# Projecting ten row tiles in five pairs with seven block products instead of eight

## The chip, the cores and the metric

The kernel runs on one core of one Trainium2 chip. A core has five engines that run side by side, each with its own queue of instructions: TensorE (PE, matrix products; its loading of weights is listed as PEld), VectorE (DVE), ScalarE (ACT), GpSimd (POOL) and SyncE (SP), which here issues most of the DMAs. Matrix products are written to PSUM, eight banks of 512 f32 columns on 128 partitions; everything else lies in SBUF. All data here are f32.

The metric is the device time of one execution in microseconds. All times below are microseconds unless they are marked ns.

## The reference

There are 16 sequences. Each has 100 rows `x` of 640 values and 722 context rows of 384 values; the last four context rows are the extra tokens. With 8 heads of 80 values the reference computes, per sequence:

```python
enc, ca = ctx[:, :718, :], ctx[:, 718:, :]
hs   = mha(x @ Wq, enc @ Wk, enc @ Wv)           # main attention
q1   = einsum('btc,th->bch', ca, Wq_ca)[:, indices]   # 100 of 384 rows
h1   = mha(q1, x, x)                             # "first" softmax of the side branch
hs2  = mha(h1 @ Wq, ca @ Wk_ca, ca @ Wv_ca)      # "second" softmax, four keys
out  = (hs + hs2) @ Wout + b_out + x
```

The last line is what the change is about: 1600 rows of 640 values times a 640 x 640 matrix.

## The kernel before

**Batches.** The loop at line 1233 runs over the 16 sequences `b`. A batch makes the scores of its 718 keys in three groups of two blocks (`scores`, line 629), their maximum over all keys (`larger`, `Maximum`), then `st - max` and the exponentials in three parts (`subtract`, `exponential`), the sums of the exponentials (`r_ps`, line 1413), their inverse (`divide`, line 976) and the values (`a_ps`, line 1431). Inside the same batch the keys of the next one (`Keys`, line 487, and `last_keys`, line 619) and the values of this one (`Values`, line 444) are projected. Both already use a block scheme with fewer products, for which GpSimd prepares thirteen sums of the next encodings (`enc_sums`, line 515). Every odd batch also makes the queries of the next two (`queries`, line 565).

**The side branch** is the class `Second` (line 761). `scores1` makes 100 x 800 scores on GpSimd in `e1` with the help of a scratch tile `product`; `softmax1` takes their maximum on VectorE in steps (transpose, reduce, four small reductions twice, copy, transpose) and subtracts it; `exponentials1` is ScalarE's; `softmax2`, `scores2` and `softmax3` follow in the next batch. `spread2` sends the 32 probabilities of a row through DRAM so that they come back spread over all partitions in `pb`, and `values2` (line 912) multiplies and adds them on GpSimd to `hs2`.

**The output.** The 1600 rows are cut into 13 tiles: eleven of 128 rows, one of 64 and one of 128 (`OC`, line 33). A tile's rows, transposed, are collected in `hsT_r` (five chunks of 128 values by 128 rows), because a batch has 100 rows and a tile 128; `ENDS` (line 36) holds the batch in which a tile's last row is made. One batch later `place` (line 1026, GpSimd) multiplies by the inverse and adds `hs2`, `add_bias` adds the bias to the tile's rows of `x` in `xn`, and `project` (line 1051) makes two halves of 320 columns from five chunks each, ten matmuls of 128 x 128 by 128 x 320. VectorE adds the result to `xn`, SP stores it. `O_AFTER` (line 37) says for each tile after which batch it is projected: tiles 0 to 9 in batches 2, 3, 4, 6, 7, 8, 10, 11, 12 and 14. The last three tiles are done in batch 15 and after the loop.

**Order.** From line 1232 on the order of every engine's instructions, SP's DMAs among them, is the order of the program text (`manual_schedule`); before that, in the preparation, a scheduler orders them by when they are ready. An engine runs its queue in order, so an instruction that waits holds up all behind it. `wait_for(ins, seen)` makes an instruction wait for the last maximum of the batch.

**Room.** `xT` (transposed `x` of two batches), `ca`, `mb` and `ys` (four small or middle tiles of the side branch) have two buffers, `hsT` two, `xn` two, `pb` one and `product` one. PSUM is used in three sets of two: `ps2` (pairs of banks, `pair`), `psk` and `ps1`. `most` (128 x 800) holds the running maximum of the scores; its rows from 96 on are set to a low value once and then overwritten up to row 120.

These lines stand at the end of a batch before the change:

```python
        if 0 < b < B - 2:
            enc_sums(enc_next)
        if b % 2 and b + 1 < B:
            ...
                queries(p + 1, xT, tiles, n)
        if 0 < b < B - 1:
            second.exponentials1()
```

Ahead of them, in the branch of batches 1 to 14, stand `last_keys`, the load of the rest of the encodings, `second.softmax1()` and `last.project()`; behind them come the matmuls of `r_ps`, `divide`, the matmuls of `a_ps` and `keep`.

Of the kernel before, what the change touches and what calls it, by code (L numbers as in the profile page):

```python
# [33 lines left out]


ENDS = [(lo + n - 1) // S for lo, n in OC]
O_AFTER = [b + 1 if b % 2 == 0 and b + 1 not in ENDS else b for b in ENDS]
HT = NH * T


# [113 lines left out]
def kernel(  # L154
# [73 lines left out]
    def load_x(p):  # L228
        xT = inp.tile([P, 2, HC, S], F32, tag="xT", name=f"xT_{p}")
        nc.sync.dma_start(  # L230
            out=xT, in_=xt[2 * p : 2 * p + 2].rearrange("b p c s -> p b c s")
        )
        return xT
# [46 lines left out]
    kT = const.tile([P, HC, 3, KT], F32, name="kT")  # L280
    wout_sb = const.tile([P, HC, H], F32, name="wout_sb")
    bias = const.tile([P, H], F32, name="bias")

    wvca_sb = enc_tile("wvca").rearrange("p f k -> p (f k)")[:, : CC * H].rearrange(
        "p (c n) -> p c n", c=CC
# [34 lines left out]
    xT = inp.tile([P, 2, HC, S], F32, tag="xT", name="xT_0")  # L320
    in_order(nc.sync.dma_start(out=xT, in_=xt[0:2].rearrange("b p c s -> p b c s")))
    ca_0 = small.tile([S, T, S], F32, tag="ca", name="ca_0", bufs=2)
# [69 lines left out]
    e1 = const.tile([P, ROWS], F32, name="e1")  # L392
    nc.gpsimd.memset(e1[96:, :], LOW)

    ys = []
    for j in range(2):
        y = const.tile([S, NH, HT + 1], F32, name=f"y_{j}")
        nc.gpsimd.memset(y[:, :, HT:], 1.0)
        ys.append(y)


    def first_values(i, enc, engines, halves=(0, 1), get=psum):
# [335 lines left out]
    def load_m(b, behind=None):  # L738
        if b < 2:
            return lambda c: m_sb[c][:, b * HT : (b + 1) * HT]  # L740
        mb = small.tile([P, HC, HT], F32, tag="mb", name=f"mb_{b}", bufs=2)
# [19 lines left out]
    class Second:  # L761


        def __init__(self, b, xT, ca=None):
            self.b, self.xT = b, xT[:, b % 2]
            self.top = None

            self.ca = ca
            if ca is not None:
                return  # L770
            self.ca = small.tile([S, T, S], F32, tag="ca", name=f"ca_{b}", bufs=2)
            nc.sync.dma_start(
                out=self.ca, in_=cas[b].unsqueeze(0).to_broadcast([S, T, S])
            )
# [24 lines left out]

        def copy(self):  # L800
            b, y_ps = self.b, self.y_ps
            self.y = ys[b % 2]
# [109 lines left out]
        def values2(self, behind=None):  # L912

            b = self.b
            pb = self.pb.rearrange("p c (t q) -> p c t q", t=T)
            self.hs2 = hs2_tile(f"hs2_{b}")[:, : HC * S].rearrange("p (c q) -> p c q", c=HC)
            for t in range(T):
                to = self.hs2
                if t:
# [3 lines left out]
                first = nc.gpsimd.tensor_tensor(  # L923
                    to, pb[:, :, t], va.to_broadcast([P, HC, S]), ALU.mult
                )
                if t:
                    nc.gpsimd.tensor_tensor(self.hs2, self.hs2, to, ALU.add)  # L927
# [9 lines left out]
    spare = []  # L937

    class Last:

# [5 lines left out]
        def load(self, behind=None):  # L946

            self.xn = {}
            for r, (lo, n) in enumerate(OC):
                if self.b != O_AFTER[r]:  # L950
                    continue
                xn = self.xn[r] = spare[1] if r == len(OC) - 1 else xn_tile(f"xn_{r}")
                rows = x.rearrange("b s n -> (b s) n")[lo : lo + n]
# [91 lines left out]
        def put(self):  # L1045
            for to, o_ps, o_v in self.due:
                nc.vector.tensor_tensor(to, o_ps, to, ALU.add)
                nc.sync.dma_start(out=o_v, in_=to)
            self.due = []

        def project(self, halves=(0, 1), apart=False, put=True):
            for r, xn in self.xn.items():
# [180 lines left out]
    for b in range(B):  # L1233
# [40 lines left out]
        nc.vector.tensor_tensor(most[:KN], st[0][:, 0], st[0][:, 1], ALU.max)  # L1274
        st.append(scores(b, 1, tiles))
# [12 lines left out]
        if b == 0:  # L1288
# [25 lines left out]
            keys(m_next)  # L1314
            enc_sums(enc_next)
            now.values2()
            second.softmax1(4)
        elif b + 1 < B:
            vv = Values(b, e_in)

            def both(n):
                vv.go(n)
                kk.go(n)

            second.scores1(seen)
            last.load(seen)
            if b + 2 < B:
                m_next = load_m(b + 2, seen)
                keys(m_next)
# [36 lines left out]
            if b + 2 < B:  # L1366
                enc_next = load_rest(b + 2, enc_next)
            second.softmax1()
            last.project()
        else:  # L1370
            vv = Values(b, e_in)
            last.place()
            last.load()
            mine.load()
            last.add_bias(seen)
            top.go(3)
            vv.go(3)
# [12 lines left out]
            vv.go(5)  # L1390
            last.put()
            vv.go(1)
            subtract(1)
            exponential(2)
            vv.go(1)
            exponential(1)
            vv.go(5)
        if 0 < b < B - 2:
            enc_sums(enc_next)
        if b % 2 and b + 1 < B:  # L1400
            xT, tiles = xT_at[0], queries_tiles(p + 1)
            for n in range(HC):
                queries(p + 1, xT, tiles, n)
        if 0 < b < B - 1:
            second.exponentials1()

        rests = psum1(f"r_ps_{b}")[:, : 2 * S].rearrange("p (e q) -> p e q", e=2)
# [33 lines left out]
            mine.keep(wides)  # L1441
        else:
            mine.finish(wides)
        if b == 0:
            second.softmax1()
            second.exponentials1()
        last = mine

    last.project(apart=True)
# [50 lines left out]
```

## Time and profile before

| what | us |
|---|---|
| median of three runs | 934.5 (933.68 to 935.29) |
| the profiled execution itself | 933.61 |
| its span in the trace | 931.9 |
| even batch with a projection (from `s_ps` to `s_ps`) | 52.9 |
| odd batch with queries, without a projection | 56.0 |
| odd batch with queries and a projection | 61.4 |

The span runs from the first to the last instruction in the trace; the execution's own time has 1.7 more around it. The lengths of batches are differences between the starts of the first scores in the chain in order of time (381.17 to 434.10, 325.16 to 381.17 and 434.10 to 495.49).

How to read the lines of the profile that follow. A line of the groups has the source line, the engine, the operation, output<-inputs, shapes, the count, the busy time in all and the mean of one in ns, then the engine's idle time before it and what ended most of that. A line of the timeline has start, length, engine, line, operation and shapes; the square bracket is the idle time of the engine just before, and what ended it. A line of the chain in order of time has start, length, engine and group, merged over neighbours. SPq is SP's queue of DMA issues. "x20" at a matmul counts instructions; a product of f32 matrices is two of them, each with its weight load.

### The profile page before, as it was taken

To read this page: it belongs to the slowest core of one execution; us is meant where nothing else is said; L and a number is where in the kernel's file an instruction comes from. 1 tells how busy PE (TensorE), PEld (TensorE's weight loads), DVE (VectorE), ACT (ScalarE), POOL (GpSimd) and SP (SyncE) were. 2 spreads that over 40 slices of the span, in tenths; PEclk is the share of its full clock that TensorE was granted. 3 is DMA by queue.
4 is the path that set the end of the run, shared out by engine and by line. 5 is a ranking of instruction groups with operands and counts; after the bars stand their busy time and mean duration, and the time that the engine had idled before them with its cause. 6 is when DMAs were issued, how large, how long until landed. Compare 5 with 4: busy or idle time off the path is not lost.

```text
span 931.9 us, 26041 instructions
## 1 busy us (share of the span) xinstructions
PE 923.7 (99%) x11183; PEld 784.3 (84%) x11183; DVE 650.8 (70%) x1087; ACT 375.4 (40%) x649; POOL 573.3 (62%) x622
## 2 busy tenths in 40 slices
PE   9999999999999999999999999999999999999998
PEld 6997879788897888988788887987889888897865
DVE  3848894886919678495955959578592876939583
ACT  2234534434334344533425434344532444434350
POOL 5649857576645865467682666756665566556444
PEclk9999999999999999999999999999999999999999
DMA  8712262051400504132131411314131050401212
GB/s 258 241 39 67 54 129 72 20 145 29 108 26 23 144 12 109 29 83 74 35 106 30 112 45 42 76 25 130 44 98 36 19 146 15 107 14 50 63 52 64
DMA packets 68667, 69.16 MB, mean 74 GB/s; under 512 B 26056, under 2 KB 62344, under 8 KB 68552
## 3 DMA queue, kind: packets, MB, share of 16 engines
q1 hardware_dynamic: 67224, 66.18, 26.9%
q8 instruction: 88, 1.44, 0.7%
q10 hardware_dynamic: 864, 0.98, 0.3%
q0 software_dynamic: 464, 0.34, 0.1%
q14 instruction: 27, 0.22, 0.1%
HBM read 61.81 MB, written 8.94 MB: 76 GB/s over the span
## 4 chain that ended last, share of the span: by engine, by line
PE 96%; DVE 2%; DMA 1%; issue 0%; ACT 0%; POOL 0%; SPq 0%; DVEq 0%; ACTq 0%
PE s_ps L643 12%; PE v_psA L468 10%; PE v_psB L468 8%; PE kT_ps L593 8%; PE k_psA L499 7%; PE q_ps L569 7%; PE a_ps L1431 7%; PE o_ps L1061 7%; PE k_psB L499 6%; PE r_ps L1413 4%; PE v_psC L468 3%; PE k_psC L499 3%; PE v_ps L409 2%; PE y_ps L782 2%; PE v_psD L468 2%; PE v_psE L468 2%
## 5 line engine op out<-in xcount | busy, mean ns | idle before, releaser
L817 POOL TENSOR_TENSOR e<-ca,g 100x800 f32<-100x800 f32 x64 | 99.4, 1564 | 156.8 <-DVE most L1263 140.4
L534 POOL TENSOR_TENSOR enc<-enc 128x240 f32<-128x240 f32 x135 | 96.5, 725 | 21.6 <-DMA enc<-in_enct 14.6
L468 PE MATMUL v_psA<-wv_sb,enc 128*120 128x320 f32 x352 | 109.6, 434 | 0.2 <-ACT st L671 0.2
L923 POOL TENSOR_TENSOR hs<-pb,vaT 128x500 f32<-128x500 f32 x64 | 73.0, 1150 | 53.7 <-DMA pb<-wide_d 51.2
L643 PE MATMUL s_ps<-qp,kT 32*120 32x100 f32 x3072 | 97.9, 263 | 0.0
L643 PEld LDWEIGHTS s_ps<-qp,kT 32*120 32x120 f32 x3072 | 95.0, 180 | 2.1 <-issue 0.2
L824 POOL TENSOR_TENSOR e<-e,e 100x800 f32<-100x800 f32 x48 | 90.6, 1887 | 3.8
L468 PE MATMUL v_psB<-wv_sb,enc 128*120 128x320 f32 x296 | 91.9, 433 | 0.0
L499 PE MATMUL k_psA<-enc,wk_sb 128*128 128x240 f32 x360 | 87.9, 367 | 1.1 <-DVE kT L439 1.0
L1274 DVE TENSOR_TENSOR most<-st 120x800 f32<-120x800 f32 x16 | 17.6, 1100 | 100.8 <-ACT st L671 100.8
L1251 DVE TENSOR_TENSOR st<-st,over 120x1600 f32<-120x1600 f32 x47 | 85.3, 1814 | 0.0
L499 PEld LDWEIGHTS k_psA<-enc,wk_sb 128*128 128x128 f32 x360 | 68.3, 190 | 18.0 <-DVE kT L439 1.3
L468 PEld LDWEIGHTS v_psA<-wv_sb,enc 128*120 128x120 f32 x352 | 63.4, 184 | 22.4 <-DVE vs L439 0.5
L1263 DVE TENSOR_TENSOR most<-most,st 120x800 f32<-120x800 f32 x64 | 65.7, 1027 | 22.8 <-ACT st L665 21.6
L1259 ACT ACTIVATE st<-st 120x1600 f32<-120x1600 f32 x48 | 73.9, 1540 | 8.2 <-DVE st L1251 7.7
L499 PE MATMUL k_psB<-enc,wk_sb 128*128 128x240 f32 x300 | 73.1, 367 | 0.1
L468 PEld LDWEIGHTS v_psB<-wv_sb,enc 128*120 128x120 f32 x296 | 54.3, 184 | 21.7 <-DVE vs L439 0.4
L1028 POOL TENSOR_TENSOR hsT<-hsT,ratio 128x500 f32<-128x500 f32 (+22 forms) x26 | 20.5, 788 | 83.0 <-DVE st L1251 74.0
L927 POOL TENSOR_TENSOR hs<-hs,hs 128x500 f32<-128x500 f32 x48 | 68.0, 1416 | 3.8
L1431 PE MATMUL a_ps<-st,vs 120*64 120x100 f32 (+1 forms) x1536 | 69.5, 250 | 0.0
L569 PE MATMUL q_ps<-xT,wq_sb 128*128 128x200 f32 x400 | 69.1, 333 | 0.0
L1431 PEld LDWEIGHTS a_ps<-st,vs 120*64 120x64 f32 (+1 forms) x1536 | 66.4, 137 | 2.7 <-issue 2.4
(166 smaller groups left out, 1854.2 us busy)
## 6 DMA issues: line engine op xcount, KB each, us to landing
pb<-p_d SPq DMA_DIRECT2D x32, 400.0 KB
enc<-in_enct SPq DMA_DIRECT2D x30, 240.0 KB
enc<-in_enct SPq DMA_DIRECT2D x15, 360.0 KB
xT<-in_xt SPq DMA_DIRECT2D x8, 500.0 KB
rest<-in_enct SPq DMA_DIRECT2D x31, 120.0 KB
xn<-in_x SPq DMA_DIRECT2D x11, 320.0 KB
wide_d<-p_d SPq DMA_DIRECT2D x16, 200.0 KB
pb<-wide_d SPq DMA_DIRECT2D x16, 200.0 KB
```

Of the source, the lines that this page charges most:

```text
L468: nc.tensor.matmul(at[0][j][:KN, : H // 2], a_form(self.enc, f)[:, j * KN : (j + 1) * KN], wv_there.get(f, wv_sb[:, W_AT[f]]), start=first ...
L499: nc.tensor.matmul(at[:, i * KT : (i + 1) * KT], wk_sb[:, W_AT[f], i], a_form(self.enc, f), start=(first and i == 0), stop=last, skip_grou ...
L534: nc.gpsimd.tensor_tensor(out, left, right, op)
L569: nc.tensor.matmul(q_ps[:, : 2 * S].rearrange("p (j s) -> p j s", j=2), wq_sb[:, c, n * P : (n + 1) * P], xT[:, :, c, :], start=(c == 0), ...
L593: nc.tensor.matmul(bank[:, i * KT : (i + 1) * KT], weights[c], a_raw(enc, u, c), start=(i == 0 and c == 0), stop=(c == CC - 1), skip_group ...
L643: nc.tensor.matmul(s_ps[bank][:n, 256 * a + lo : 256 * a + lo + rhs.shape[-1]], kT[rows, c, u, j * KN : (j + 1) * KN], rhs, start=bank not ...
L817: first = nc.gpsimd.tensor_tensor(to, self.ca[:, t, :].unsqueeze(1).to_broadcast([S, NH, S]), g[:, :, t].unsqueeze(2).to_broadcast([S, NH, ...
L824: nc.gpsimd.tensor_tensor(e, e, to, ALU.add)
L923: first = nc.gpsimd.tensor_tensor(to, pb[:, :, t], va.to_broadcast([P, HC, S]), ALU.mult)
L1251: return engine.tensor_tensor(st[i], st[i], top.over[:KN].unsqueeze(1).to_broadcast([KN, 2, ROWS]), ALU.subtract,)
L1259: nc.scalar.activation(st[i], st[i], AF.Exp, scale=SCALE)
L1431: nc.tensor.matmul(wides[64 * e : 64 * e + 64, h // 2], slot(i, h, FIRST[e], 64), st[i // 2][: KEYS[i], i % 2, h * S : (h + 1) * S], start ...
```

## The change

It does four things.

1. **Pairs.** Tiles 0 to 9 are projected as five pairs, in batches 3, 6, 8, 11 and 13, the batch after the second tile's last row. With the two tiles' first four chunks as a 2 x 2 block matrix `A` and the first four chunks of `Wout` as a 2 x 2 block matrix `B`, Winograd's form of Strassen's scheme needs seven block products instead of eight; the fifth chunk is done as before. The sums of blocks of `A` are made per pair on GpSimd (`row_sums`, right behind `place`), into the room of `most` and in place; the sums of blocks of `B` once on VectorE (`out_sums`, at the end of batch 1), three into a new tile and one in place, whose block is loaded again in batch 14 (`again`).
2. **The block itself** (`project_pair`) uses a pair of banks and two single ones. VectorE adds partial sums to `xn` in the middle of the sums; in even batches the steps of `softmax1` are put between these additions. At its end GpSimd sets the rows of `most` again, ahead of `enc_sums`.
3. **Room.** `xT`, `ca`, `mb` and `y` get one buffer, `product` lies in the room of `pb`, `values2` works in place, `hsT` gets three buffers.
4. **Order.** The stores of a pair are kept and issued in the next batch behind its last maximum, ahead of that batch's load of `xn`. In even batches without a pair the second half of `softmax1` comes behind `keep`, and `exponentials1` in the next batch behind the first group of scores, as it was in batch 0.

```diff
-O_AFTER = [b + 1 if b % 2 == 0 and b + 1 not in ENDS else b for b in ENDS]
+NPAIRS = 5
+O_AFTER = [ENDS[r | 1] - (r + 1) % 2 for r in range(2 * NPAIRS)] + ENDS[2 * NPAIRS :]
+PAIRED = {ENDS[r + 1]: (r, r + 1) for r in range(0, 2 * NPAIRS, 2)}
...
-        return main.tile([P, HC, P], F32, tag="hsT", name=name, bufs=2)
+        return main.tile([P, HC, P], F32, tag="hsT", name=name, bufs=3)
...
-        xT = inp.tile([P, 2, HC, S], F32, tag="xT", name=f"xT_{p}")
+        xT = inp.tile([P, 2, HC, S], F32, tag="xT", name=f"xT_{p}", bufs=1)
...
-            self.ca = small.tile([S, T, S], F32, tag="ca", name=f"ca_{b}", bufs=2)
+            self.ca = small.tile([S, T, S], F32, tag="ca", name=f"ca_{b}")
...
-                    to = product_tile(f"hs2_{b}_{t}")[:, : HC * S]
-                    to = to.rearrange("p (c q) -> p c q", c=HC)
+                to = pb[:, :, t] if t else self.hs2
...
     def product_tile(name):
-        return main.tile([P, ROWS], F32, tag="product", name=name)
+        return pb_tile(name)[:, :ROWS]
+    def out_sums():
+        (b11, b12), (b21, b22) = w_there
+        for out_w, left, right in (
+            (wout_t[:, 0], b12, b11),
+            (b12, b22, b12),
+            (wout_t[:, 1], b22, wout_t[:, 0]),
+            (wout_t[:, 2], b21, wout_t[:, 1]),
+        ):
+            nc.vector.tensor_tensor(out_w, left, right, ALU.subtract)
...
+        def row_sums(self):
+            t0, t1 = (hsTs[r] for r in PAIRED[self.b])
+            room = most[:, : 6 * P].rearrange("p (i c s) -> p i c s", i=3, c=2)
+            self.s1, self.s2, self.s4 = (room[:, i] for i in range(3))
+            a11, a12, a21, a22 = t0[:, :2], t0[:, 2:4], t1[:, :2], t1[:, 2:4]
+            for to, left, right, op in (
+                (self.s1, a21, a22, ALU.add),
+                (a21, a11, a21, ALU.subtract),
+                (self.s2, self.s1, a11, ALU.subtract),
+                (self.s4, a12, self.s2, ALU.subtract),
+            ):
+                nc.gpsimd.tensor_tensor(to, left, right, op)
+        def project_pair(self, steps):
...
+            step()
+            product(y, t0[:, :2], b11, True)
+            product(z, t1[:, :2], t3, True)
+            add(x0[:, 0], y[:, : H // 2])
+            step()
+            product(y, self.s2, tt2)
+            add(x1, both[:, :, : H // 2])
+            step()
+            product(v, t0[:, 2:4], b21, True)
+            rest(v, t0, 0)
+            product(y, self.s1, tt1)
+            add(x0[:, 1], y[:, : H // 2])
+            step()
+            product(z, t1[:, 2:4], tt4)
+            rest(z, t1, 0)
+            add(x1[:, 0], z[:, : H // 2])
+            step(8)
+            product(w, self.s4, b22, True)
+            rest(w, t0, 1)
+            rest(y, t1, 1)
+            add(x0[:, 0], v[:, : H // 2])
+            add(x0[:, 1], w[:, : H // 2])
+            add(x1[:, 1], y[:, : H // 2])
+            nc.gpsimd.memset(most[96:, :], LOW)
+            held.extend((r, xns[r]) for r in (r0, r1))
...
             second.scores1(seen)
+            store(seen)
             last.load(seen)
+            if b == B - 2:
+                again()
...
             last.place(subtract(1))
+            if last.b in PAIRED:
+                last.row_sums()
             last.add_bias()
...
-            second.softmax1()
-            last.project()
...
-        if 0 < b < B - 2:
-            enc_sums(enc_next)
+        paired = 0 < b and last.b in PAIRED
+        late = b % 2 == 0 and not paired
+        if b < B - 1 and (b % 2 or late):
+            second.softmax1(4 if late else 8)
...
-        if 0 < b < B - 1:
+        if paired:
+            last.project_pair(None if b % 2 else second.softmax1)
+        if 0 < b < B - 2:
+            enc_sums(enc_next)
+        if b < B - 1 and not late:
             second.exponentials1()
...
-        if b == 0:
+        if b == 1:
+            out_sums()
+        if late and b < B - 1:
             second.softmax1()
-            second.exponentials1()
```

`product` and `rest` in `project_pair` are two matmuls over the two chunks of a block and one over the fifth chunk, each 128 x 128 by 128 x 320; `add` is one VectorE addition from PSUM into `xn`; `t3` is the block changed in place.

More of the change, by code (lines that the diff above doesn't have):

```diff
@@ L282 @@
     bias = const.tile([P, H], F32, name="bias")
+    wout_t = const.tile([P, 3, 2, H // 2], F32, name="wout_t")
+    w_there = [
+        [wout_sb[:, 2 * i : 2 * i + 2, k * (H // 2) : (k + 1) * (H // 2)] for k in range(2)]
+        for i in range(2)
+    ]
     wvca_sb = enc_tile("wvca").rearrange("p f k -> p (f k)")[:, : CC * H].rearrange(
@@ L319 @@
     load_first(0, CC, 0, slice(0, KT))
-    xT = inp.tile([P, 2, HC, S], F32, tag="xT", name="xT_0")
+    xT = inp.tile([P, 2, HC, S], F32, tag="xT", name="xT_0", bufs=1)
     in_order(nc.sync.dma_start(out=xT, in_=xt[0:2].rearrange("b p c s -> p b c s")))
-    ca_0 = small.tile([S, T, S], F32, tag="ca", name="ca_0", bufs=2)
+    ca_0 = small.tile([S, T, S], F32, tag="ca", name="ca_0")
     in_order(nc.sync.dma_start(out=ca_0, in_=cas[0].unsqueeze(0).to_broadcast([S, T, S])))
@@ L393 @@
     nc.gpsimd.memset(e1[96:, :], LOW)
[L395 to L399, printed above, removed]
+    y_there = const.tile([S, NH, HT + 1], F32, name="y")
+    nc.gpsimd.memset(y_there[:, :, HT:], 1.0)
     def first_values(i, enc, engines, halves=(0, 1), get=psum):
@@ L740, in load_m @@
             return lambda c: m_sb[c][:, b * HT : (b + 1) * HT]
-        mb = small.tile([P, HC, HT], F32, tag="mb", name=f"mb_{b}", bufs=2)
+        mb = small.tile([P, HC, HT], F32, tag="mb", name=f"mb_{b}")
         loaded = nc.sync.dma_start(
@@ L801, in copy @@
             b, y_ps = self.b, self.y_ps
-            self.y = ys[b % 2]
+            self.y = y_there
             nc.scalar.copy(
@@ L931, in product_tile, with again, store @@
     def product_tile(name):
-        return main.tile([P, ROWS], F32, tag="product", name=name)
+        return pb_tile(name)[:, :ROWS]
     hsTs = {}
     spare = []
+    def out_sums():
[7 more added lines that the diff above has]
+            nc.vector.tensor_tensor(out_w, left, right, ALU.subtract)
+    def again():
+        rows = wout.rearrange("(c e k) n -> e c k n", e=2, k=D)
+        for e in range(2):
+            nc.sync.dma_start(
+                out=w_there[0][1][64 * e : 64 * e + 64],
+                in_=rows[e, :2, FIRST[e] : FIRST[e] + 64, H // 2 :].rearrange(
+                    "c k n -> k c n"
+                ),
+            )
+    xns = {}
+    held = []
+    def store(behind):
+        while held:
+            r, xn = held.pop(0)
+            lo, n = OC[r]
+            stored = nc.sync.dma_start(
+                out=out.rearrange("b s n -> (b s) n")[lo : lo + n], in_=xn[:n]
+            )
+            wait_for(stored, behind)
     class Last:
@@ L952, in load @@
                 xn = self.xn[r] = spare[1] if r == len(OC) - 1 else xn_tile(f"xn_{r}")
+                xns[r] = xn
                 rows = x.rearrange("b s n -> (b s) n")[lo : lo + n]
@@ new lines, in project_pair, with product, rest, add @@
+        def project_pair(self, steps):
+            r0, r1 = PAIRED[self.b]
+            t0, t1 = hsTs[r0], hsTs[r1]
+            x0, x1 = (xns[r].rearrange("p (k d) -> p k d", k=2) for r in (r0, r1))
+            b11, t3 = w_there[0]
+            b21, b22 = w_there[1]
+            tt1, tt2, tt4 = (wout_t[:, i] for i in range(3))
+            both = pair(f"o_ps_{r0}")
+            y, z = both[:, 0], both[:, 1]
+            v, w = psumk(f"o_psv_{r0}"), psumk(f"o_psw_{r0}")
+            def product(bank, rows, weights, first=False, last=False):
+                for c in range(2):
+                    nc.tensor.matmul(
+                        bank[:, : H // 2],
+                        rows[:, c],
+                        weights[:, c],
+                        start=(first and c == 0),
+                        stop=(last and c == 1),
+                        skip_group_check=True,
+                    )
+            def rest(bank, rows, k, last=True):
+                nc.tensor.matmul(
+                    bank[:, : H // 2],
+                    rows[:, HC - 1],
+                    wout_sb[:, HC - 1, k * (H // 2) : (k + 1) * (H // 2)],
+                    start=False,
+                    stop=last,
+                    skip_group_check=True,
+                )
+            def add(to, left):
+                nc.vector.tensor_tensor(to, left, to, ALU.add)
+            def step(n=1):
+                if steps:
+                    steps(n)
+            step()
[23 more added lines that the diff above has]
+            held.extend((r, xns[r]) for r in (r0, r1))
@@ L1271 @@
         st.append(scores(b, 0, tiles))
-        if b == 0:
+        if b == 0 or late:
             now.exponentials1()
@@ L1316 @@
             now.values2()
-            second.softmax1(4)
         elif b + 1 < B:
@@ L1443 @@
             mine.finish(wides)
-        if b == 0:
+        if b == 1:
+            out_sums()
+        if late and b < B - 1:
             second.softmax1()
-            second.exponentials1()
         last = mine
```

2 lines of the change are left out of this document (removed).

## The prediction

> **What bounds the kernel now.** I read the page first, then the groups of instructions, then the chain in order of time, and last the timeline of single batches.
>
> ```profile
> span 931.9 us, 26041 instructions
> PE 923.7 (99%) x11183; PEld 784.3 (84%) x11183; DVE 650.8 (70%) x1087; ACT 375.4 (40%) x649; POOL 573.3 (62%) x622
> PE 96%; DVE 2%; DMA 1%; issue 0%; ACT 0%; POOL 0%; SPq 0%; DVEq 0%; ACTq 0%
> ```
>
> TensorE is busy for 99% of the span and holds 96% of the chain that ended last. A busy PE alone proves little, because ends of matmuls are modelled; the chain in order of time is better, since it shows when each group starts:
>
> ```profile
> 313.29 5.38 PE o_ps L1061 x20
> 318.67 2.21 PE r_ps L1413 x96
> ...
> 362.57 3.65 PE kT_ps L593 x18
> 366.22 8.46 PE q_ps L569 x50
> 374.68 2.22 PE r_ps L1413 x96
> ...
> 418.58 3.65 PE kT_ps L593 x18
> 422.23 5.38 PE o_ps L1061 x20
> ```
>
> Groups follow each other without a gap: 313.29 + 5.38 = 318.67, where `r_ps` starts. In batch 4 the projection is in that row, in batch 5 none stands between the keys and `r_ps` (only queries), in batch 6 it is there again. So whatever TensorE no longer does should come off the span, as long as the other engines keep up with the shorter batches.
>
> **The change, part by part.** *Products removed.* One tile costs 20 instructions (an f32 matmul is two) in 5.38, so one takes 5.38 / 20 = 0.269. Two tiles had 2 x 2 x 5 = 20 matmuls. The pair block has seven products of two chunks and four for the fifth chunk: 18. That is 36 instructions of the same form for 40, 36 x 0.269 = 9.68 instead of 10.76. Five pairs: 5 x 1.08 = **5.38 less**. Ten batches' blocks become five (batches 3, 6, 8, 11, 13), so batches 3, 6, 8 and 11 grow by 9.68 - 5.38 = 4.30 and 13 by 9.68, and batches 2, 4, 7, 10, 12 and 14 lose 5.38.
>
> *Handovers added.* Bank `y` is read by VectorE three times while TensorE goes on summing in it. This is new, so I lay the block into batch 6, the even case, where the steps of the softmax stand between the additions:
>
> ```profile
> 417.31 1.81 DVE L1251 TENSOR_TENSOR st<-st,over 120x1600 f32<-120x1600 f32 x1
> 419.04 1.00 DVE L706 STREAM_TRANSPOSE turned<-e 128x800 f32<-128x800 f32 x1
> 420.08 0.99 DVE L708 TENSOR_REDUCE quad<-turned 128x25 f32<-128x800 f32 x1
> 421.10 0.71 DVE L711 TENSOR_REDUCE side<-quad 32x25 f32<-32x25 f32 x4
> 421.85 1.32 DVE L718 TENSOR_REDUCE mx<-side 32x25 f32<-32x100 f32 x4
> 423.20 0.99 DVE L733 COPY spread<-mx 128x800 f32<-128x800 f32 x1
> 424.22 1.01 DVE L736 STREAM_TRANSPOSE over<-spread 128x800 f32<-128x800 f32 x1
> 425.26 0.99 DVE L834 TENSOR_TENSOR e<-e,over 100x800 f32<-100x800 f32 x1
> 427.72 0.82 DVE L1074 TENSOR_TENSOR xn<-o_ps,xn 128x640 f32<-128x640 f32 x1 [1.46 <-PE o_ps L1061]
> L1047 DVE TENSOR_TENSOR xn<-o_ps,xn 128x320 f32<-128x320 f32 x2 | 1.0, 488 | 0.8 <-PE o_ps L1061 0.8
> 89.40 1.08 PE L499 MATMUL k_psA<-enc,wk_sb 128*128 128x240 f32 x4 [0.97 <-DVE kT L439]
> 88.70 0.65 DVE L439 TENSOR_TENSOR kT<-k_psA,kT 128x480 f32<-128x480 f32 x1
> ```
>
> From matmul to addition: the projection ends at 427.61 and the addition starts at 427.72, 0.11 later; the last matmul's ending is modelled, so I allow 0.3. An addition of 320 columns takes 0.49, of 640 columns 0.82. From VectorE back to TensorE: the addition ends at 88.70 + 0.65 = 89.35, the matmul that waited starts at 89.40, 0.05 later. The block starts at 422.23. `y` is done at 423.31 and `z` at 424.38. VectorE has finished its first step at 420.04, so it adds `y` until 423.31 + 0.3 + 0.49 = 424.10, and TensorE may write `y` again at 424.15: 0.23 to spare, or none if the weights of that matmul must wait too, one instruction (0.27) ahead. Then VectorE's second step lasts to 425.1; `y` is done at 425.46, both banks are added until 426.6, and TensorE, with six instructions in `v`, comes back to `y` at 427.07: 0.4 to spare. The third step (2.0) ends at 428.6 and the third addition at 429.1; TensorE needs `y` again at 431.4 and `z` was free from 426.6. In odd batches no step stands between. So the cost lies between 0 (all fits) and 0.3 a pair (the allowance at the first point doubled); VectorE is idle when `y` comes, so I take a value near 0: 0.05 a pair, 0.25 in all.
>
> The rest of VectorE's work there is hidden by TensorE: its steps end at 432.6 and the three last additions at 434.1, before the inverse, which follows `r_ps` (431.9 + 2.2 = 434.1). ScalarE's exponential at 432.6 (0.87 long) is also done before that. Without this cover the additions would cost 1.5 a pair.
>
> *Less cover in batches 2, 4, 10, 12 and 14.* With the block gone, `r_ps` starts at 313.29 in batch 4. It needs the third pair of scores in its last third, at 313.29 + 2/3 x 2.21 = 314.8:
>
> ```profile
> 308.37 1.81 DVE L1251 TENSOR_TENSOR st<-st,over 120x1600 f32<-120x1600 f32 x1
> 310.28 1.54 ACT L1259 ACTIVATE st<-st 120x1600 f32<-120x1600 f32 x1
> ...
> 104.84 1.24 POOL L927 TENSOR_TENSOR hs<-hs,hs 128x500 f32<-128x500 f32 x1
> 105.08 1.85 DVE L1274 TENSOR_TENSOR most<-st 120x800 f32<-120x800 f32 x1 [2.53 <-ACT st L671]
> 161.84 0.99 DVE L1274 TENSOR_TENSOR most<-st 120x800 f32<-120x800 f32 x1 [6.20 <-ACT st L671]
> ```
>
> The exponential ends at 311.82, so 3.0 remain. Moving the second half of the softmax behind `divide` puts 1.01 + 0.99 of VectorE into the 6.20 in which it waits for the next scores, and its exponential (0.87) between two groups of ScalarE's copies of them; a bank is copied some 0.1 later. Cost 0, and 0.1 a batch at most.
>
> *GpSimd.* Four sums of 128x256 a pair, near the 128x260 row (0.74), make 2.9; the fill of `most` counts as a fifth, 0.74.
>
> ```profile
> L1028 POOL TENSOR_TENSOR hsT<-hsT,ratio 128x260 f32<-128x260 f32 x1 | 0.7, 740 | 5.3 <-DVE st L1251 5.3
> 419.47 2.02 POOL L923 TENSOR_TENSOR hs<-pb,vaT 128x500 f32<-128x500 f32 x2 [3.24 <-DMA pb<-wide_d]
> 427.22 1.27 POOL L927 TENSOR_TENSOR hs<-hs,hs 128x500 f32<-128x500 f32 x1
> 783.66 3.04 POOL L817 TENSOR_TENSOR e<-ca,g 100x800 f32<-100x800 f32 x2 [7.98 <-DVE most L1263]
> ```
>
> In batch 6 the sums fit into the 3.24 in which GpSimd waits for the spread probabilities. The fill waits for TensorE's last product (431.9), and behind it are queued the thirteen sums of the next encodings; they start at 432.7 instead of 428.5, where `values2` ends, 4.2 later. TensorE's next batch, and with it the maximum that `scores1` waits for, comes 4.3 later too, so that wait stays as it is. In an unpaired even batch the least wait before `scores1`, 7.98, shrinks by 5.38 to 2.6. So all of it costs 0; uncovered it would be 3.6 a pair. GpSimd and VectorE do hold each other up: `most` took 1.85 beside GpSimd's sum at 104.84 and 0.99 alone. Against a cost of 0 speaks a rule of the Trainium skill, page SBUF — State Buffer, section Who interferes with whom: a VectorE instruction with two inputs in SBUF and a GpSimd one that reads SBUF exclude each other for a whole instruction. By it the moved subtraction (0.99) would hold GpSimd up once a batch, and 1.6 of the 2.6 would remain, so the sum is the same and only the GpSimd rival below gains weight. The trace agrees, by the two rows of `most`.
>
> *Weight sums*, once, behind batch 1: four of 128x640, twice the 0.49 of 320 columns, so 3.9, or by the factor of the two rows of `most` (1.85 / 0.99) up to 7.3, of which the 6.20 before 161.84 hold all but 1.1; that 1.1 would make `scores1` late once, within the 7.98. Cost 0; without that cover 3.9 once.
>
> *Single buffers.* In the loop `xT`, `ca`, `mb` and `y` are written only after their last reader has long run, since that reader stands earlier in the same batch. `product` shares `pb`, whose other users are on the same GpSimd queue or follow it. The stores come behind the next maximum, two of them, ahead of `xn` and `mb`; `mb` is needed only after `scores1`, some 12 later. Cost 0. The start is different:
>
> ```profile
> 41.52 0.52 SPq L230 DMA_DIRECT2D xT<-in_xt  x1
> 42.09 0.40 SPq L772 DMA_DIRECT2D ca<-in_cas  x1
> 51.59 28.75 SPq L246 DMA_DIRECT2D enc<-in_enct  x6
> 78.63 1.72 SPq L246 DMA_DIRECT2D enc<-in_enct  x3
> 57.44 0.69 POOL L534 TENSOR_TENSOR enc<-enc 128x240 f32<-128x240 f32 x1 [14.56 <-DMA enc<-in_enct]
> 68.47 1.21 PE L782 MATMUL y_ps<-m,xT 128*100 128x96 f32 x10
> 80.21 1.54 POOL L817 TENSOR_TENSOR e<-ca,g 100x800 f32<-100x800 f32 x1
> 85.75 0.69 POOL L534 TENSOR_TENSOR enc<-enc 128x240 f32<-128x240 f32 x1
> 113.46 3.03 POOL L817 TENSOR_TENSOR e<-ca,g 100x800 f32<-100x800 f32 x2 [3.68 <-DVE most L1263]
> ```
>
> Now `xT_1` waits for the last reader of `xT_0` (to 69.68) and `ca_2` for that of `ca_1` (to 81.75). Batch 2's encodings, the second three of the six at 51.59, queue behind: from 78.6 to about 82.2. The first encodings took 57.44 - 51.59 = 5.9, so sums that start at 85.75 wait to about 88, 2.3 of the 3.68 that are free. Cost 0. TensorE's 0.97 of waiting at 89.40 lies in this stretch and may go or double, so -1 to +1 for the range.
>
> *The sum*, against the profiled execution's own 933.61 (its span 931.9 and 1.7 around it): 933.61 - 5.38 + 0.25 = 928.5. The median of the runs, 934.5, is 0.9 above that execution, so I predict **929.4**.
>
> **The rivals.** *A. The handovers take the gain back.* If VectorE answers a step late at two places of a block (0.3 and 0.5), a pair loses 0.8 and the five 4.0: 933.4. For it: the first handover has 0.23 or less. Against: VectorE is idle before it.
>
> *B. Slower: batch 1's encodings fall behind `xT_1` in SP's queue.* In the trace `xT` and `ca` stand ahead of them, at 41.52 and 42.09. If that order stays while `xT_1` waits to 69.68, the encodings leave 18.1 late, and their thirteen sums start at 75.5 and end some 10 later. TensorE wants them from 69.7 on, and GpSimd's `scores1`, queued behind all of them, makes the softmax behind it late: some 15 lost, 929.4 + 15 = 944. It decides as soon as the load of `enc_1` is issued after 69. Against: those loads stood behind only because their own buffer came free at 51.6, which is now earlier than the others' are.
>
> *C. GpSimd sets the pace in unpaired even batches.* If VectorE instructions that it did not meet before held it up for 4 in all (four of about 1.0), 1.4 beyond the reserve would be lost in each of five: 936.4. For it: 2.6 is the smallest reserve, and the rule above. Against: nothing of its work is added there.
>
> *D. No shorter block.* If 36 instructions with interrupted sums took the time of 40 (0.299 each), the gain would be nil: 934.7. Against: same shapes and same pitch.
>
> **How the numbers follow.** Forecast 0.78, A 0.09, B 0.06, C 0.04, D 0.03. About 0.2% (1.9 us: 932.6 to 936.4) is what a measurement can tell from no change. Faster is the forecast and a third of A: 0.81. Same is the rest of A and D: 0.09. Slower is B and C, as C's own 936.4 is the edge: 0.10. The forecast's own range is 928.2 (the wait at 89.40 gone) to 930.8 (it doubled, with 0.1 a pair); up to 932.4 it takes in the milder part of A.
>
> **What would show it.** Right: projection rows of 36 instructions in about 9.7, five times, with at most 0.3 of idle PE inside; kT followed directly by `r_ps` in batches 2, 4, 10, 12 and 14 with no wait for an exponential; `scores1` still waiting for `most` everywhere, by 2 to 3 after those batches; `enc` loads issued near 52 at the start. Wrong: PE waiting for `xn` additions by more than 0.3, `p2t` on VectorE waiting for `p_in` by more than now, or a first batch that is longer.

## The result, and the profile after

| kernel | median us | range | runs |
|---|---|---|---|
| before | 934.09 | 933.02 to 935.29 | 4 |
| after | 940.15 | 939.93 to 940.48 | 4 |

The ratio is 1.0065 with a 95% interval of 1.0047 to 1.0082: the change made the kernel slower by 6.1, where 5.1 less was forecast. The page of the changed kernel, its span, engines and the chain that ended last:

```profile
span 938.2 us, 26084 instructions
PE 921.5 (98%) x11163; PEld 777.7 (83%) x11163; DVE 660.2 (70%) x1116; ACT 374.8 (40%) x649; POOL 611.8 (65%) x646
PE 91%; DVE 6%; ACT 1%; issue 1%; POOL 0%; DVEq 0%; POOLq 0%; ACTq 0%
```

TensorE has 20 instructions fewer and is busy 2.2 less, but the chain has passed from TensorE to VectorE by some per cent. First, where: the starts of the first scores in the chain in order of time, before and then after.

```profile
157.60 7.28 PE s_ps L643 x240
210.85 7.28 PE s_ps L643 x240
272.24 7.28 PE s_ps L643 x240
```

```profile
157.63 7.28 PE s_ps L650 x240
205.17 7.28 PE s_ps L650 x240
273.34 7.28 PE s_ps L650 x240
```

Batch 2 takes 47.54 instead of 53.25, as it should (-5.71). Batch 3, with a pair block, takes 68.17 instead of 61.39: +6.78, where +4.30 was forecast. All batches, by what the change does in them, as differences from before. The column of the forecast holds the products alone, without the allowance of 0.25; the last two columns are experiments told below.

| stretch | forecast | after | two tiles | two tiles, `over` later |
|---|---|---|---|---|
| up to the first scores | 0 | +0.1 | -0.1 | -0.3 |
| batches 3, 6, 8, 11, 13 (pair blocks) | +26.9 | +38.1 | +29.3 | +27.9 |
| batches 2, 4, 7, 10, 12, 14 (a tile less) | -32.3 | -31.8 | -31.5 | -31.8 |
| batches 0, 1, 5, 9, 15 | 0 | -0.1 | +1.2 | -0.8 |
| span | -5.4 | +6.3 | -1.0 | -5.0 |

Of the 11.7 that are missing, 11.2 lie in the batches with a pair block. The chain of the changed kernel through the block of batch 3:

```profile
255.41 2.17 PE o_ps L1118 x8
258.23 1.31 PE o_ps L1118 x4
...
261.16 1.09 PE o_ps L1118 x4
262.82 1.34 PE o_ps L1118 x4
...
266.86 2.21 PE r_ps L1540 x96
```

From 255.41 to 266.86 it takes 11.45, not 9.68. The other four take 11.65, 11.62, 11.45 and 11.45: 57.6 in all, **9.2 more** than 48.4. There are two holes: 2.17 of products started at 255.41, but the next ones come at 258.23, and 261.16 + 1.09 is 262.25, but the next come at 262.82. The timeline of the block of batch 6 says what ends them, first TensorE, then VectorE:

```profile
418.52 2.32 PE L1118 MATMUL o_ps<-wout_sb,hsT 128*128 128x320 f32 x8
421.51 1.31 PE L1118 MATMUL o_ps<-wout_t,most 128*128 128x320 f32 x4 [0.68 <-DVE xn L1138]
...
426.30 1.34 PE L1118 MATMUL o_ps<-wout_t,hsT 128*128 128x320 f32 x4 [0.78 <-DVE xn L1138]
...
430.26 1.94 PE L1540 MATMUL r_ps<-st,vs 120*32 120x100 f32 x80
420.87 0.49 DVE L1138 TENSOR_TENSOR xn<-o_ps,xn 128x320 f32<-128x320 f32 x1 [4.09 <-PE o_ps L1118]
...
422.93 0.82 DVE L1138 TENSOR_TENSOR xn<-o_ps,xn 128x640 f32<-128x640 f32 x1 [0.68 <-PE o_ps L1118]
...
425.75 0.49 DVE L1138 TENSOR_TENSOR xn<-o_ps,xn 128x320 f32<-128x320 f32 x1
```

The eight instructions of the first row are four for `y` and four for `z`. `y` is complete in their middle, near 419.7, and VectorE has been idle for 4.09; yet its addition of `y` starts at 420.87, 0.03 after the end of `z` (418.52 + 2.32). Then TensorE waits for that addition. The second hole is stranger: the products that start at 426.30 go into `z`, whose only reader so far, the addition of both banks, ended at 423.75. They wait for the addition at 425.75, which reads `y`. Both holes look as if the two banks were one.

What TensorE waited for in all (each row: us in total, times, longest), after:

```profile
PE o_ps L1118 <- DVE xn L1138: 6.7, 10, 0.8
PE k_psE L506 <- DVE vs L446: 1.5, 3, 0.8
PE z_ps L851 <- issue: 1.4, 2, 0.9
```

and in the kernel before, the only one of these there:

```profile
PE k_psE L499 <- DVE vs L439: 0.5, 1, 0.5
```

The first row is the two holes of the five blocks. It adds up to 6.7 and not to 9.2, because a last matmul is shown 0.43 long while the next one in an unbroken row starts 0.27 after it, and because the first matmul behind a wait takes up to 0.1 longer. `k_psE` is a bank of the next batch's keys, `v_psE` (read by the additions into `vs`) one of this batch's values, and `z_ps` holds the sums behind the side branch's first softmax. These two rows are smaller, and neither was in the forecast. With 9.2, the 1.0 by which `k_psE` waited longer and the 1.4 of `z_ps` make 11.6 of the 11.7.

The remaining steps of the prediction answer to these rows: the DMA issues of the start, GpSimd's waits there and ahead of `scores1`, TensorE's wait at the start, and a batch without a block.

```profile
51.70 2.37 SPq L251 DMA_DIRECT2D enc<-in_enct  x2
...
69.81 0.37 SPq L235 DMA_DIRECT2D xT<-in_xt  x1
82.06 0.32 SPq L779 DMA_DIRECT2D ca<-in_cas  x1
88.01 0.96 POOL L541 TENSOR_TENSOR enc<-enc 128x240 f32<-128x240 f32 x1 [2.11 <-DMA enc<-in_enct]
217.74 3.04 POOL L824 TENSOR_TENSOR e<-ca,g 100x800 f32<-100x800 f32 x2 [2.10 <-PE v_psD L475]
669.19 3.04 POOL L824 TENSOR_TENSOR e<-ca,g 100x800 f32<-100x800 f32 x2 [1.08 <-ACT vs L448]
89.04 1.08 PE L506 MATMUL k_psA<-enc,wk_sb 128*128 128x240 f32 x4 [0.50 <-DVE kT L446]
195.04 3.65 PE kT_ps L600 x18
198.69 2.21 PE r_ps L1540 x96
```

### The profile page after: what moved, and what is told of

Read it like the earlier page. It is cut to its first block, busy times and chain, and to the rows that moved or that the text cites. A ratio compares the mean times of both kernels' runs of the same rounds, so it can differ in the third digit from the quotient of the medians.

```text
span 938.2 us, 26084 instructions
## 1 busy us (share of the span) xinstructions
PE 921.5 (98%) x11163; PEld 777.7 (83%) x11163; DVE 660.2 (70%) x1116; ACT 374.8 (40%) x649; POOL 611.8 (65%) x646
## 3 DMA queue, kind: packets, MB, share of 16 engines
q8 instruction: 88, 1.44, 0.7%
## 4 chain that ended last, share of the span: by engine, by line
PE 91%; DVE 6%; ACT 1%; issue 1%; POOL 0%; DVEq 0%; POOLq 0%; ACTq 0%
PE s_ps L650 12%; PE v_psA L475 10%; PE v_psB L475 8%; PE kT_ps L600 8%; PE a_ps L1558 7%; PE q_ps L576 7%; PE k_psA L506 7%; PE k_psB L506 6%; PE r_ps L1540 4%; PE v_psC L475 3%; PE o_ps L1118 3%; PE k_psC L506 3%; PE y_ps L789 2%; PE v_ps L416 2%; DVE most L1382 2%; PE v_psD L475 1%
## 5 line engine op out<-in xcount | busy, mean ns | idle before, releaser
L541 POOL TENSOR_TENSOR enc<-enc 128x240 f32<-128x240 f32 x135 | 109.8, 823 | 19.7 <-ACT qp L584 10.1
L1382 DVE TENSOR_TENSOR most<-most,st 120x800 f32<-120x800 f32 x64 | 69.6, 1088 | 21.8 <-ACT st L672 20.7
L576 PEld LDWEIGHTS q_ps<-xT,wq_sb 128*128 128x128 f32 x400 | 67.9, 190 | 0.2
L678 ACT COPY st<-s_ps 120x800 f32<-120x800 f32 x64 | 49.7, 829 | 43.9 <-PE s_ps L650 43.9
```

Source lines behind the costliest of these rows:

```text
L541: nc.gpsimd.tensor_tensor(out, left, right, op)
L576: nc.tensor.matmul(q_ps[:, : 2 * S].rearrange("p (j s) -> p j s", j=2), wq_sb[:, c, n * P : (n + 1) * P], xT[:, :, c, :], start=(c == 0), ...
L1382: most_now = nc.vector.tensor_tensor(most[:KN], most[:KN], st[i][:, u], ALU.max)
```

## The experiments

The theory, T1: TensorE and VectorE hand the accumulators over by the tile, and `y` and `z` are the two banks of one tile, so each waits for the other's work. The rival, T2: the way from TensorE to VectorE and back is slow by itself.

**Two tiles.** `y` and `z` get a tile each, nothing else moves; the addition that read both banks becomes two.

```diff
-            both = pair(f"o_ps_{r0}")
-            y, z = both[:, 0], both[:, 1]
+            y, z = bank(f"o_psy_{r0}"), psum1(f"o_psz_{r0}")
...
-            add(x1, both[:, :, : H // 2])
+            add(x1[:, 0], y[:, : H // 2])
+            add(x1[:, 1], z[:, : H // 2])
```

> Theory T1: a pair block loses time at two places because `y` and `z` lie in one tile of two banks and the waits go by the whole tile: VectorE's first addition of `y` starts only after the last product of `z` (0.84 us a block), and the last products of `z` wait for the third addition of `y` (0.75 to 0.95). With `y` and `z` in two tiles both go: 5 x (0.84 + 0.85) = 8.4 off 940.15, so 931.7, between 930.5 and 933.5; a block from the first o_ps to r_ps is 9.7 to 10.0 us instead of 11.45 to 11.65. Theory T2: the handover from TensorE to VectorE and back is what is slow, whichever tile the bank belongs to: the block stays at 11 us or more, and the time between 938 and 941 (one more addition on VectorE a block).

Measured: 931.08 (930.25 to 932.57, nine runs) against 934.05 before; ratio 0.9969, interval 0.9959 to 0.9979. The block of batch 6 again, TensorE and then VectorE (this profiled execution took 932.57, the longest of the nine):

```profile
417.47 1.24 PE L1117 MATMUL o_psy<-wout_sb,hsT 128*128 128x320 f32 x4
...
419.62 1.24 PE L1117 MATMUL o_psy<-wout_t,most 128*128 128x320 f32 x4
...
427.25 1.93 PE L1540 MATMUL r_ps<-st,vs 120*32 120x100 f32 x80
418.75 0.49 DVE L1137 TENSOR_TENSOR xn<-o_psy,xn 128x320 f32<-128x320 f32 x1 [3.02 <-PE o_psy L1117]
```

VectorE now adds `y` at 418.75, while `z` is being made, and TensorE returns to `y` at 419.62 without a wait. The block takes 427.25 - 417.47 = 9.78, where it took 430.26 - 418.52 = 11.74. In the chain in order of time all five blocks take 9.69, where they took 11.45 to 11.65. T1 holds, with its number (931.7 was expected); T2 falls.

The traces also show the waits themselves. In all five blocks of the changed kernel the first signal that TensorE gives to VectorE stands on the eighth instruction, the last product of `z`, and none on the fourth, the last of `y`. With two tiles it stands on the fourth. The weight load at 426.29 of the changed kernel, a product of `z`, carries a wait for VectorE's semaphore. So the holes are waits that the program itself sets.

**One tile, the addition split.** The control: the two-tile kernel also split an addition.

```diff
-            add(x1, both[:, :, : H // 2])
+            add(x1[:, 0], y[:, : H // 2])
+            add(x1[:, 1], z[:, : H // 2])
```

> The changed kernel, `y` and `z` still in one tile, and only the second addition of the block split into one for `y` and one for `z`, as the kernel with two tiles also has it. Theory T1 (waits go by the tile): both stalls stay, five blocks of 11.4 to 11.9 us, 940.2 (939.5 to 941.5). Rival: the split alone gave what the kernel with two tiles gained (TensorE need no longer wait for a long addition over two banks): 931 to 935.

Measured: 941.08 (940.78 to 941.91), ratio to before 1.0083 (1.0068 to 1.0098). Its five blocks take 11.45 to 11.71. In the timeline of batch 6 both holes are there, and the first signal of each block is again on the last product of `z`:

```profile
421.96 1.31 PE L1118 MATMUL o_ps<-wout_t,most 128*128 128x320 f32 x4 [0.68 <-DVE xn L1138]
...
426.80 1.34 PE L1118 MATMUL o_ps<-wout_t,hsT 128*128 128x320 f32 x4 [0.83 <-DVE xn L1138]
```

So the tile is what counts, not the length of the addition.

**Eight products.** The pairs, the room, the stores and the order of the change stay; each pair is multiplied the plain way, every bank read only when it is finished.

```diff
-            product(y, t0[:, :2], b11, True)
-            product(z, t1[:, :2], t3, True)
...
+            whole(y, t0, 0)
+            whole(z, t0, 1)
+            add(x0, both[:, :, : H // 2])
+            whole(v, t1, 0)
+            add(x1[:, 0], v[:, : H // 2])
+            whole(w, t1, 1)
+            add(x1[:, 1], w[:, : H // 2])
```

> All of the change (room, kept stores, the order of the batches, two row tiles at once) but eight plain products a pair instead of seven, so 40 instructions and no bank that is read between its products; the row sums, the weight sums and the second load of the weights go. If the stalls inside the block hold the loss: a block is 40 x 0.269 = 10.8 us instead of 11.5, so 5 x 0.75 = 3.8 off 940.15, 936.4; that is 2.3 above before, which is what the order and the room cost. If the loss lies in the order and the room, and the seven products do save their 5.4: 945.5.

Measured: 936.52 (935.63 to 937.64), ratio 1.0027 (1.0016 to 1.0038). As the first theory has it: its blocks take 10.77 in the chain, so with its holes the block of 36 instructions was slower than one of 40. Without holes it is faster: the kernel with two tiles, 931.08, is 5.4 below this one, which is what the forecast gave for the removed products. The run also says that about 2.5 of the loss belongs to something other than the block. Its rows of waits:

```profile
PE k_psE L506 <- DVE vs L446: 1.6, 3, 0.9
PE z_ps L851 <- issue: 1.3, 3, 0.7
```

Before, the first row was 0.5 and the second was not listed, so the two hold about 2.4.

**Room alone**, in the kernel before: single buffers for `xT`, `ca`, `mb` and `y`, three for `hsT`, `product` in the place of `pb`, the values summed in place.

```diff
-        xT = inp.tile([P, 2, HC, S], F32, tag="xT", name=f"xT_{p}")
+        xT = inp.tile([P, 2, HC, S], F32, tag="xT", name=f"xT_{p}", bufs=1)
...
-        return main.tile([P, ROWS], F32, tag="product", name=name)
+        return pb_tile(name)[:, :ROWS]
```

> The kernel before with only the room of the change: one buffer for xT, ca, mb and y, three for hsT, the product of the weights in the place of pb, the second values summed in place. My prediction put this at 0 in the loop and -1 to +1 at the start: 934.1, between 933.1 and 935.1. If the room costs part of the 2.3 that the block leaves open: 935 to 936.5.

Measured: 933.44 (932.72 to 935.59), ratio 0.9996 (0.9986 to 1.0006). The room is free. That leaves the order, with the kept stores, and the stalls of `z_ps`, which are taken up at the end.

**The softmax early.** Which part of the order? My first guess was the softmax of the side branch, which unpaired even batches take behind `divide`.

```diff
-        late = b % 2 == 0 and not paired
-        if b < B - 1 and (b % 2 or late):
+        late = b == 0
+        if b < B - 1 and (b % 2 or not paired):
```

> The unpaired even batches 6, 8 (and all others but batch 0) take the softmax and the exponentials of the second batch before the queries instead of after the last product. If this late order is what makes TensorE wait in the following odd batches (for the scale of the second half of the keys, 1.45 in sum, and the unexplained stalls of z_ps, 1.9): 936.8. If these losses come from elsewhere: 940.2, or up to 943 if the early exponentials now wait in the batches without a pair block ahead of them.

Measured: 941.13 (941.02 to 941.91), ratio to before 1.008 (1.0064 to 1.0095); 940.15 was the changed kernel. Taking the softmax early gains nothing, and the guess fell: the trace still has k_psE waiting in batches 1, 3, 5, 11 and 13. All of them except batch 1 follow a batch that has lost its projection.

**Cover given back.** So the two-tile kernel got products that feed nothing in batches 2, 4, 10 and 12, where a projection had stood.

```diff
+        elif 0 < b < B - 2 and b % 2 == 0:
+            idle_ps = psum1(f"idle_ps_{b}")
+            for c in range(20):
+                nc.tensor.matmul(
...
```

> The kernel with two tiles, and 20 products of 128 x 320 more (5.38 us, they feed nothing) in each of the batches 2, 4, 10 and 12, where the kernel before projects a tile and the changed one none. Theory C (less cover: VectorE enters the next odd batch with work left over because TensorE has none of the projection's time in between): the waits of k_psE in batches 3, 5, 11 and 13 go (3.05), 931.1 + 4 x 5.38 - 3.05 = 949.6. Rival (the waits come from the next batch's own order): they stay, 952.6.

Measured, one run: 972.79, span 971.1. I had counted 20 products as 20 instructions; they are 40, 10.76 a batch, 43.0 in all. Against the span of 930.9 with two tiles that is 973.9, and 2.8 less came out; but that span belongs to the longest of nine runs, 1.5 above their median, so the sum alone proves little. The row of the waits does not need the sum; with two tiles alone, then with cover:

```profile
PE k_psE L506 <- DVE vs L446: 2.6, 5, 0.7
```

```profile
PE k_psE L506 <- DVE vs L446: 0.7, 1, 0.7
```

Only batch 1 still waits, as it did before the change. So the time in which TensorE had been projecting had let VectorE catch up; without it VectorE enters the next odd batch late. The cover given back was twice what had been taken away; that 5.38 would have been enough is not shown.

**`over` behind the additions.** What is VectorE late for? In the kernel before, batch 3:

```profile
230.41 1.00 DVE L736 STREAM_TRANSPOSE over<-spread 128x800 f32<-128x800 f32 x1
231.33 0.85 DVE L439 TENSOR_TENSOR vs<-v_psE,vs 120x320 f32<-120x320 f32 x2
...
232.19 0.97 PE L499 MATMUL k_psE<-enc,wk_sb 128*128 128x240 f32 x4
```

k_psE starts at 232.19, as the additions that read v_psE end (231.33 + 0.85): it was only just on time. With two tiles, batch 5, the same three rows:

```profile
340.39 1.00 DVE L743 STREAM_TRANSPOSE over<-spread 128x800 f32<-128x800 f32 x1
341.31 0.85 DVE L446 TENSOR_TENSOR vs<-v_psE,vs 120x320 f32<-120x320 f32 x2
341.82 1.08 PE L506 MATMUL k_psE<-enc,wk_sb 128*128 128x240 f32 x4 [0.61 <-DVE vs L446]
```

The transposition `over`, 1.00 long, stands ahead of the additions for which k_psE waits. The experiment swaps them:

```diff
             both(2)
+            vv.go(1)
             top.go()
-            both(2)
+            vv.go(1)
+            kk.go(2)
```

> The kernel with two tiles (931.08), and in every batch VectorE's transposition `over` stands behind the additions of v_psE instead of ahead of them. There k_psE waited for these additions by 0.57 to 1.0 in batches 1, 3, 5, 11 and 13 (3.9 in sum), in before by 0.75 in batch 1 alone. Theory: VectorE is late there by its own order, and nothing that follows `over` is as late: 931.08 - 3.9 = 927.2. Rival: `over` and the exponentials behind it come 0.85 later in every batch and the wait comes back at the exponentials and the sums a_ps: 930 to 935.

Measured: 928.43 (928.12 to 929.27, four runs) against 933.61 before; ratio 0.9947, interval 0.993 to 0.9964. The median is 2.65 below that of the two-tile kernel, or 2.1 by the ratios to before, where 3.9 was expected; the row of the waits had 2.6. The rival's 930 to 935 was not reached. No wait of k_psE is left, and batch 1, which had it before the change too, is shorter by 0.7 than before. Batch 5:

```profile
338.53 0.88 DVE L446 TENSOR_TENSOR vs<-v_psE,vs 120x320 f32<-120x320 f32 x2
...
339.46 0.97 PE L506 MATMUL k_psE<-enc,wk_sb 128*128 128x240 f32 x4
```

This kernel is faster than both that were given. What the swap alone would give the kernel before, whose row has 0.5, was not run.

**The instructions shifted.** In the last loss, `z_ps`, TensorE waits for nothing that the profile shows. In the changed kernel, batch 10, with the view of the DMA queues from 614 to 617 (40 slices of 0.075):

```profile
615.27 0.73 PE L851 MATMUL z_ps<-y,e 100*32 100x33 f32 x61
616.92 0.23 PE L851 MATMUL z_ps<-y,e 100*32 100x33 f32 x3 [0.92 <-issue]
DMA  0000000700000000000000000000000000000000
q8 instruction: 1, 0.02, 2.0%
```

One packet of the instruction queue, near 614.6, and TensorE stands from 616.0 until 2.3 after it. To tell an instruction fetch from a wait for data, 40 tiny products at the very start move the stream by 160 instructions, half of them weight loads.

```diff
+    for _ in range(40):
+        nc.tensor.matmul(
+            idle_ps[:32, :33], idle[:100, :32], idle[:100, :33], start=True, stop=True
+        )
```

> The kernel with two tiles, and 40 tiny products more (32 x 33, about 0.01 us each) ahead of the first loads, which feed nothing: they shift TensorE's stream of instructions by 80. Theory F: z_ps (64 products and 64 loads in 0.53 us) stalls where its instructions have not been fetched; every such stall ends 2.3 to 2.8 us after a packet of the instruction queue. Then the stalls leave batches 2, 8 and 10 (0.84, 0.25, 0.68) for other batches, and still end 2.3 to 2.8 after such a packet; time 929.3 to 932.5. Rival: z_ps waits for its data or its bank: the stalls stay in batches 2, 8 and 10, time 931.1 to 931.6.

Measured: 933.05 (932.37 to 934.46). The stalls left batches 2, 8 and 10, and one appeared in batch 5 (view of the DMA queues from 383 to 386, same slices):

```profile
384.71 0.75 PE L851 MATMUL z_ps<-y,e 100*32 100x33 f32 x62
385.98 0.22 PE L851 MATMUL z_ps<-y,e 100*4 100x33 f32 x2 [0.52 <-issue]
DMA  0000000070000000000000000000000000000000
```

The packet is at 383.6, the stall ends 2.4 later. In the ten traces of this study 27 stalls of z_ps above 0.1 (by the starts of its weight loads) end between 2.27 and 2.83 after such a packet; two short ones of them, 0.30 and 0.16, are in the kernel before. Other groups of z_ps run through such a time without a stall. That the place follows the stream speaks for the fetch, and no run shows it directly. The time missed its range: the tiny products took 3.58 rather than 0.5 and put the first scores 1.5 later (61.96 for 60.46). That a shift makes the kernel faster was not shown.

## Why the prediction was wrong

*Products removed, -5.38:* right. With two tiles each of the five blocks lasts 9.69 in the chain (for 9.68), the kernel with eight products has 10.77, and the two kernels lie 5.4 apart; batches that lost a tile are shorter by 31.8 of the 32.3 that were forecast.

*Handovers added, 0.25:* **this step failed, and it turned the sign.** It said that VectorE "adds `y` until 423.31 + 0.3 + 0.49 = 424.10", counting from the end of `y`, and that `z` "was free from 426.6". Both took bank `y` and bank `z` for separate accumulators. The line `both = pair(...)` makes them one tile, and the program's waits are set for the tile: the addition starts after `z`, and `z` waits for a reader of `y`. The lags came out shorter in sum than I allowed (0.03 from product to addition and 0.15 back, for 0.3 and 0.05); what was wrong is what they were counted from. Cost 9.2 for five blocks, 1.84 a pair, against 0.05. The waits are signals that the program sets, as the traces show; that neighbouring banks might also disturb each other in some other way was not tried, since in the two-tile kernel `z` lies in another set of banks. The Trainium skill, page PSUM — Partial Sum Buffer, section "PSUM bank collisions raise a hardware error", has accumulators guarded by the bank. The two-tile kernel, which waits by the bank and stands still nowhere in its five blocks, agrees. In its batch 6 the first addition ends at 419.24 (418.75 + 0.49), 0.38 ahead of TensorE's return, where 0.23 was worked out.

*Less cover, 0 to 0.1 a batch:* this term was put too low, because it looked at one batch alone. I asked what the shorter batch itself needs early, the exponentials for `r_ps`, and there it holds: keys from 195.04, `r_ps` from 198.69, 3.65 later and without a gap. I did not ask what the following batch needs. There VectorE had nothing in hand ahead of k_psE. In the changed kernel such waits rose from 0.5 to 1.5, with two tiles to 2.6.

*GpSimd, 0:* right. The wait ahead of `scores1` stayed everywhere, with 2.10 to 2.35 and once 1.08 where 2.6 was forecast (1.6 with the moved subtraction in GpSimd's way); at the start it waits 2.11 at 88.01, for 2.3 worked out. *Single buffers, 0:* right by the run of the room alone; at the start `xT` is issued at 69.81 and `ca` at 82.06, as worked out, and the wait at 89.04 is 0.50 for 0.97.

*Not in the prediction:* the stalls of z_ps, 1.4 in the row of waits. *A slip in the range:* its upper end, 930.8, comes to 930.6 from its own terms (929.4 + 0.97, and 0.25 more for the handovers), which changes nothing here.

*The rivals.* A came nearest, with VectorE answering late at two places of a block, at 0.8 a pair; the price was 1.84, because it looked for a slow VectorE and not for a wait set too wide. B fell: the encodings are issued at 51.70, ahead of `xT`. C fell: GpSimd kept a reserve. D fell: with two tiles the 36 instructions take 9.69, with their sums interrupted as before and without the waits.

## What to carry to other kernels

Before costing a handover between engines, look up which tile each bank belongs to: an accumulator that is read while a neighbour is still being summed needs a tile of its own. When work is taken out of a stage, look one stage further, at each row that was on time by less than the work removed, and count from there. If a block comes out longer than its instructions, ask of every hole not only which engine was waited for, but which of its instructions, and whether that one touches the same data.

## What the runs showed of the hardware

TensorE seems to run short of instructions in places. z_ps is 64 products and 64 loads in some 0.5, and at 27 places in ten traces it stood still for 0.11 to 1.14 and went on 2.27 to 2.83 after a packet of the instruction queue (88 packets and 1.44 MB in a run, 16 KB each). The Trainium skill, page Runtime: NRT & Kernel Launch, section "Instruction fetch mechanics", gives the 16 KiB blocks and calls the cost of crossing one mostly hidden. If these stalls are the fetch, as the shifted stream suggests, it was not hidden in this dense run of tiny products, by up to 1.14 at a time.
